# A six-layer transformer stack on one core: the score mask copied into PSUM by ScalarE, and a written order of half steps

## The chip, the cores and the metric

The kernel runs on one core of a Trainium2 chip. The core has five engines that run beside each other, each through its own queue in order: TensorE (PE in the profile, with PEld for its weight loads), VectorE (DVE), ScalarE (ACT), GpSimd (POOL) and SyncE (SP), which here only issues DMAs. Matmuls write to PSUM; DVE and ACT read and write PSUM and SBUF, POOL works in SBUF alone. The metric is the device time of the whole program in microseconds (us), smaller is better.

## The reference, cut to what matters

The input is `x` of 16 sequences, 256 tokens, 128 features, float32. First comes one causal attention layer with 16 heads of 8 features, added to `x` (called stage 1 below; the change does not touch it, apart from the constants that it prepares). Then a layernorm and a stack of six layers, whose result is added again:

```python
for i in range(6):
    x = attn_layer(shift_tokens(x), Wqkv[i], q_scale[i], k_scale[i], Wo[i]) + x
    x = ffn_layer(shift_tokens(x), ln_g[i], ln_b[i], W1[i], b1[i], W2[i], b2[i]) + x
```

`shift_tokens` takes half of the features from the token before. `attn_layer` has 16 heads of 64 features: queries and keys are divided by their norms, scaled and rotated (rotary tables with a decay), and each block of 32 tokens attends to itself and to the block before, under a mask:

```python
sim = einsum('bhwie,bhwje->bhwij', bq, bk2) * 8.0
sim = where(mask, -finfo.max, sim)
out = einsum('bhwij,bhwje->bhwie', softmax(sim, -1), bv2)
```

`ffn_layer` is a layernorm, a product with `W1` (128 to 682), a gated gelu and a product with `W2` (341 to 128). All matmuls of the stack are in float32.

## The kernel before, in words

**Work units.** The stack runs over `n = 16 * layer + sequence`, 96 values. For each `n` there are two half steps, `u = 0` and `u = 1`, each for half of the 16 heads. The function `half(n, u)` writes down one half step; 192 of them follow each other. It is a software pipeline: one half step holds parts of several `n` and of the feed-forward net (the "glu") of an earlier pair of sequences `m`. The glu works on two sequences at once and its parts are spread over four half steps, so the pattern repeats every four half steps. They are called here E0 (n even, u = 0), E1 (n even, u = 1), O0 and O1 (n odd).

**What a half step does.** Per half step, with `i, j` the two quarters of 4 heads that belong to `u`, and `b` the half of heads whose softmax weights are ready:

- `proj_qk` for `n + 2` (twice, each with q and k): two matmuls, ACT squares the result (L495), DVE multiplies by the rotary tables (L496, 128x1024). Then POOL adds the squares (L505) and the rotary halves (L508, two of 128x512), all behind the second of the pair.
- in u = 0: `norms` for `n + 1` (column sums of the squares, PE), an ACT copy, then `roots` (a PE transpose and a chain of 12 small DVE operations), POOL spreads the result (`kb`, L542).
- `spread_k` and `norm_k`, for two of four head groups each: PE transposes `kb` into PSUM, DVE scales the keys (L567, two), and SP issues four DMAs of 256 KB that lay q and k out anew (`us`, L569).
- `masks`: eight bf16 matmuls write the additive mask into the score tile in PSUM (L594), and `sim` adds the scores for four head groups onto it (L614, `start=False`). `soften` scales the scores and takes the row maximum (DVE, L626 and L634), and POOL subtracts it (L635).
- `power` takes the exponential (ACT, L641), half a step later `share` sums the rows and divides (DVE L648, L649; L651 on POOL, and on DVE where i is 1), `attn_T` transposes the weights (PE, L657) with an ACT copy (L659), `attn_v` multiplies by the values (PE, L677) with an ACT copy of the result (L686), and `project_out` closes the attention (PE L697, DVE L702).
- `proj_v` (PE L577, ACT L583), twice, with DMAs that lay the values out shifted by a block (`vs`, L584 and L586).
- glu: `glu_shift` (POOL), `glu_center`, `glu_var`, `glu_turn`, `glu_norm` and three `glu_part` (gelu on ACT, L797; product on DVE, L799), `glu_out` (PE L808, DVE L810).

**Order.** Each step function issues its instructions for all engines, and `in_order` then ties every PE, DVE, ACT and POOL instruction behind the one written before it on that engine. So each of the four engines runs exactly in the order in which `half` calls the steps. SP is not tied; the tile framework places the DMAs.

**Buffers.** PSUM has eight banks. Four are the pool `ps_o` (`psum1`): each result of a projection, transpose, norm or glu product takes one, and PE waits when all four are still to be read. The other four are two tiles of two banks (`ps_s`, `psum2`), which the scores and the attention result take in turn. In SBUF the buffers that matter are those with few copies: `t12` and `sq2` (2), `tq` (6), `us` and `sm` (3), `ao` and the value tiles (1 for each u), and the glu's scratch (1 each).

**Weights** of a layer are loaded at the step that first uses them: `load_qk` and `load_tables` (a DMA of 1 MB and two POOL operations, L436) in `proj_qk`, `load_v`, `load_out` and `load_glu` likewise.

Of the kernel before, what the change touches and what calls it, by code (L numbers as in the profile page):

```python
# [7 lines left out]
F32 = mybir.dt.float32  # L8
# [30 lines left out]
def tile_transformer(  # L39
# [35 lines left out]
    mask_b = const.tile([P, 2, 512], BF16, name="mask_b")  # L75
# [28 lines left out]
    with ExitStack() as st:  # L104
# [234 lines left out]
        def for_stack():  # L339

            for k in range(2):
                for half in range(2):
                    for quarter in range(4):
                        r = 32 * quarter
                        col = V_QK + 2 * k + (half + quarter) % 2
                        nc.gpsimd.tensor_copy(qks[r : r + 32, :, k, half], vecs[r : r + 32, :, col])

            nc.gpsimd.tensor_copy(
                mask_b.rearrange("p a n -> p (a n)"), cst1[:, C_MASK - C_CAUS : C_MASK - C_CAUS + 1024]
            )  # L350
# [36 lines left out]
    with ExitStack() as st:  # L387
# [13 lines left out]
        ps_s = st.enter_context(tc.tile_pool(name="ps_s", bufs=2, space=PSUM))  # L401
# [67 lines left out]
        xs, sq2s, t12s, sq, tq, us, rn, kbs, ao, sims, exs, aTs, pos, xns, hs = ({} for _ in range(15))  # L469
# [11 lines left out]
        def proj_qk(n, g, k):  # L481
# [20 lines left out]
            if k == 1:  # L502
                sq[n, g] = f5.tile([P, 2, S], F32, tag="sq", name=f"sq_{n}_{g}")
                tq[n, g] = e6.tile([P, 2, 2, S], F32, tag="tq", name=f"tq_{n}_{g}")
                nc.gpsimd.tensor_tensor(sq[n, g], sq2[:, :, 0, :], sq2[:, :, 1, :], ALU.add)  # L505

                for t in range(2):
                    nc.gpsimd.tensor_tensor(tq[n, g][:, t], t12[:, :, 0, t, :], t12[:, :, 1, 1 - t, :], ALU.add)  # L508
# [14 lines left out]
        def roots(n, n2):  # L523
# [16 lines left out]
            rn[n] = y  # L540
            kb = p1.tile([P, 2, NG, P], F32, tag="kb", name=f"kb_{n}")
# [46 lines left out]
        def masks(n, u):  # L588
            ps = sims[n, u] = psum2(f"sim_{n}_{u}")
            for r in range(4):  # L590
                for x in range(2):
                    w = 2 * x + r % 2
                    row = slice(32 * w, 32 * w + 32)
                    nc.tensor.matmul(  # L594
                        ps[WIN * r : WIN * r + WIN, x, :],
                        ident_b[row, row],
                        mask_b[row, 0 if r == 0 else 1, :],
                        start=True,
                        stop=False,
                        skip_group_check=True,  # L600
                    )

        def sim(n, u, g):


            ps, qk = sims[n, u], us[n, u]
            for h in range(2):
                for r in range(4):
                    c = block(r, h)
                    first = WIN if c == 0 else 0  # L610
                    col = 128 * g + 64 * h
                    for x in range(2):
                        part = slice(64 * x, 64 * x + 64)
                        nc.tensor.matmul(  # L614
                            ps[WIN * r : WIN * r + WIN, x, col + first : col + 64],
                            qk[part, g, 0, WIN * c : WIN * c + WIN],
                            qk[part, g, 1, WIN * (c - 1) + first : WIN * (c + 1)],
                            start=False,
                            stop=True,
                            skip_group_check=True,  # L620
                        )

        def soften(n, i):
            ps = sims[n, i // 2][:, i % 2]
# [9 lines left out]
            nc.vector.tensor_reduce(mx, seg, AX.X, ALU.max)  # L634
            nc.gpsimd.tensor_tensor(seg, seg, mx.unsqueeze(2).to_broadcast([P, 8, 64]), ALU.subtract)  # L635
            sms[n, i] = sm

        def power(n, i):
            sm = sms.pop((n, i))
# [4 lines left out]
        def share(n, i):  # L644
# [4 lines left out]
            nc.vector.reciprocal(rec, rec)  # L649
            on = nc.vector if i == 1 else nc.gpsimd  # L650
# [11 lines left out]
        def attn_v(n, i):  # L662
# [23 lines left out]
            nc.scalar.copy(ao[n, u][:, x], po[:, :, x])  # L686
# [17 lines left out]
        x2s, bcs, sms = {}, {}, {}  # L704
# [123 lines left out]
        def has(n):  # L828
            return 0 <= n < N
# [9 lines left out]

        def half(n, u):  # L840
            even = n % 2 == 0
            m = n // 2 - 1 if even else (n - 3) // 2
            glu = lambda m: 0 <= m < N // 2 - 1
# [3 lines left out]
            do(b, share, bi)  # L847
            do(b, share, bj)
            do(n, sim, u, 0)
            do(n, sim, u, 1)  # L850
            for k in range(2):
                do(n + 2, proj_qk, i, k)
            if u == 0:
                do(n + 1, sums)
            else:
                do(n + 1, spread_k, 1)
                do(n + 1, norm_k, 1)
                if not even and glu(m):
                    glu_norm(m)
            do(n, sim, u, 2)  # L860
            do(n, sim, u, 3)
            do(n, soften, i)
            do(n, soften, j)
            do(n - 1, project_out, u)
            if n == N - 1 and u:
                glu_shift((N // 2 - 1, 0))
            if u:
                do(n + 3, shift)
                if even and glu(m):
                    glu_shift(m)  # L870
            elif has(n + 1):
                roots(n + 1, n2s.pop(n + 1))
            do(b, attn_T, bi)
            do(b, attn_T, bj)
            do(n, proj_v, u, 0)
            do(b, attn_v, bi)
            if n == N - 1 and u:
                do(n, power, i)
                do(n, power, j)
            if not even and u == 0 and glu(m):  # L880
                glu_center(m)
            do(n + 2, proj_qk, j, 0)
            if even and u == 0 and glu(m - 1):
                glu_part(m - 1, 2)
            if not even and glu(m):
                if u == 0:
                    glu_var(m)
                else:
                    glu_part(m, 0)
                    glu_part(m, 1)  # L890
            do(n + 2, proj_qk, j, 1)
            if not even and u == 0 and glu(m):
                glu_turn(m)
            if u == 0:
                do(n + 1, spread_k, 0)
                do(n + 1, norm_k, 0)
            if n < N - 1 or u == 0:
                do(n, power, i)
                do(n, power, j)
            do(b, attn_v, bj)  # L900
            do(*((n, masks, 1) if u == 0 else (n + 1, masks, 0)))
            if even and u and glu(m - 1):
                glu_out(m - 1)
                if m - 1 >= (DEPTH - 1) * 8:
                    leave(2 * ((m - 1) % 8))
                    leave(2 * ((m - 1) % 8) + 1)
            do(n, proj_v, u, 1)

        def tail():
# [5 lines left out]
            share(n, 2)  # L915
            share(n, 3)
# [5 lines left out]
            attn_v(n, 2)  # L922
            attn_v(n, 3)
# [127 lines left out]
```

## Time and profile before

| what | value |
|---|---|
| three runs | 3608.91, 3615.72, 3619.88 us; median 3615.72 |
| span of the profiled execution, first to last instruction | 3608.7 us |
| stage 1 and the start of the stack, to the first mask of n = 0 | some 383 us |
| one period of four half steps in mid-stack (1600.03 to 1665.71) | 65.68 us |
| busy in that period: PE, DVE, POOL, ACT | 65.03, 54.19, 51.32, 36.19 us |
| granted TensorE clock | 0.990 over the span, 1.00 in that period |

No separate device time is listed for the profiled execution; its span is 0.2 us below the fastest of the three runs and 7.0 us below their median. [...] The chain of waits follows the work back from the last instruction, and in mid-stack its PE rows lie end to end, so that each row's length is what that group costs.

### The profile page before, as it was taken

To read this page: it belongs to the slowest core of one execution; us is meant where nothing else is said; L and a number is where in the kernel's file an instruction comes from. 1 tells how busy PE (TensorE), PEld (TensorE's weight loads), DVE (VectorE), ACT (ScalarE), POOL (GpSimd) and SP (SyncE) were. 2 spreads that over 40 slices of the span, in tenths; PEclk is the share of its full clock that TensorE was granted. 3 is DMA by queue.
4 is the path that set the end of the run, shared out by engine and by line. 5 is a ranking of instruction groups with operands and counts; after the bars stand their busy time and mean duration, and the time that the engine had idled before them with its cause. 6 is when DMAs were issued, how large, how long until landed. Compare 5 with 4: busy or idle time off the path is not lost.

```text
span 3608.7 us, 153932 instructions
## 1 busy us (share of the span) xinstructions
PE 3473.3 (96%) x68101; PEld 2428.7 (67%) x68101; DVE 2837.0 (79%) x4876; ACT 1881.1 (52%) x3184; POOL 2568.1 (71%) x2729
## 2 busy tenths in 40 slices
PE   8999799999999999999999999999999999999998
PEld 6777466666666666666666666666666666666665
DVE  6665788887888888888887888887888888888884
ACT  3444255554555555555555555555555555555553
POOL 2221787777777777787777777777777877777772
PEclk9999899999999999999999999999999999999999
DMA  3000333334433334333334333334433343443342
GB/s 83 10 9 10 97 94 98 99 95 104 112 104 86 92 100 112 102 105 101 84 96 119 105 90 100 95 90 120 111 92 87 100 110 86 109 107 93 101 105 63
DMA packets 249446, 331.69 MB, mean 92 GB/s; under 512 B 74446, under 2 KB 105548, under 8 KB 247884
## 3 DMA queue, kind: packets, MB, share of 16 engines
q1 hardware_dynamic: 248060, 321.14, 34.1%
q8 instruction: 537, 8.80, 1.0%
q14 instruction: 129, 1.06, 0.1%
q10 hardware_dynamic: 720, 0.70, 0.1%
HBM read 28.14 MB, written 4.19 MB: 9 GB/s over the span
## 4 chain that ended last, share of the span: by engine, by line
PE 78%; DVE 9%; issue 7%; POOL 3%; ACT 2%; DMA 1%; SPq 0%; POOLq 0%; DVEq 0%; ACTq 0%
PE qk L494 18%; PE po L677 11%; PE v L577 9%; PE wo L697 8%; PE sim L614 7%; PE w L808 4%; PE hg L794 3%; PE ha L795 3%; PE aT L657 3%; PE n L515 2%; DVE tq L567 2%; PE bc L553 2%; PE sim L594 2%; DVE t L496 2%; ACT aT L659 1%
## 5 line engine op out<-in xcount | busy, mean ns | idle before, releaser
L496 DVE TENSOR_TENSOR t<-qk,ab 128x1024 f32<-128x1024 f32 x768 | 916.6, 1219 | 277.1 <-ACT sq L495 244.9
L508 POOL TENSOR_TENSOR tq<-t 128x512 f32<-128x512 f32 x768 | 961.4, 1273 | 87.7 <-DVE t L496 69.5
L494 PE MATMUL qk<-xs,wqk 128*128 128x256 f32 x3072 | 792.6, 394 | 1.2 <-DVE yT L702 1.2
L505 POOL TENSOR_TENSOR sq<-sq 128x512 f32<-128x512 f32 x384 | 489.1, 1274 | 339.6 <-ACT sq L495 327.3
L494 PEld LDWEIGHTS qk<-xs,wqk 128*128 128x128 f32 x3072 | 555.5, 191 | 155.6 <-issue 54.9
L495 ACT ACTIVATE sq<-qk 128x512 f32<-128x512 f32 x768 | 459.5, 598 | 352.4 <-PE qk L494 346.8
L659 ACT COPY aT<-aT 128x512 f32<-128x512 f32 x384 | 207.7, 587 | 600.3 <-PE aT L657 599.9
L677 PEld LDWEIGHTS po<-aT,vs 64*64 64x64 f32 x12288 | 327.3, 134 | 201.5 <-issue 109.1
L577 PE MATMUL v<-wv,xs 128*128 128x512 f32 x768 | 422.9, 632 | 27.8 <-ACT aT L659 21.2
L635 POOL TENSOR_TENSOR sm<-sm,mx 128x512 f32<-128x512 f32 x384 | 396.3, 1043 | 30.4 <-DVE mx L634 29.8
L677 PE MATMUL po<-aT,vs 64*64 64x32 f32 x12288 | 393.8, 222 | 7.7 <-issue 4.3
L614 PEld LDWEIGHTS sim<-us 64*32 64x32 f32 x24576 | 262.5, 105 | 205.6 <-issue 190.5
L677 PE MATMUL po<-aT,vn 64*64 64x32 f32 x12288 | 386.0, 219 | 3.3 <-issue 3.3
L583 ACT COPY vn<-v 128x512 f32<-128x512 f32 x384 | 225.3, 587 | 312.1 <-PE v L577 307.6
L697 PE MATMUL wo<-ao,wout 128*128 128x256 f32 x1536 | 382.7, 392 | 0.0
L677 PEld LDWEIGHTS po<-aT,vn 64*64 64x64 f32 x12288 | 329.6, 135 | 5.2 <-issue 5.2
L614 PE MATMUL sim<-us 64*32 64x64 f32 (+1 forms) x24576 | 324.7, 221 | 3.6 <-DMA us<-tq 3.2
L651 POOL TENSOR_TENSOR ex<-ex,rec 128x512 f32<-128x512 f32 x288 | 296.4, 1043 | 42.6 <-DVE rec L649 22.0
L697 PEld LDWEIGHTS wo<-ao,wout 128*128 128x128 f32 x1536 | 276.0, 189 | 47.4 <-issue 0.2
L686 ACT COPY ao<-po 128x512 f32<-128x512 f32 x384 | 222.9, 580 | 118.2 <-PE po L677 117.9
L648 DVE TENSOR_REDUCE rec<-ex 128x8 f32<-128x512 f32 x384 | 252.1, 656 | 32.8 <-ACT ex L641 32.8
L634 DVE TENSOR_REDUCE mx<-sm 128x8 f32<-128x512 f32 x384 | 263.5, 686 | 13.3
(145 smaller groups left out, 5206.5 us busy)
## 6 DMA issues: line engine op xcount, KB each, us to landing
us<-tq SPq DMA_DIRECT2D x768, 256.0 KB
vs<-vn SPq DMA_DIRECT2D x384, 192.0 KB
vs<-vn SPq DMA_DIRECT2D x192, 64.0 KB
wqk<-in_f_wqkv_dram SPq DMA_DIRECT2D x96, 64.0 KB
ab<-in_tables_dram SPq DMA_DIRECT2D x6, 1024.0 KB
wv<-in_f_wqkv_dram SPq DMA_DIRECT2D x12, 256.0 KB
wout<-in_f_wo_dram SPq DMA_DIRECT2D x24, 128.0 KB
x<-in_x_dram SPq DMA_DIRECT2D x16, 128.0 KB
```

What stands on the lines that cost most here:

```text
L494: nc.tensor.matmul(ps[:, t * S : t * S + S], W["qk", g][:, k, t, :], xs[n], start=True, stop=True)
L495: nc.scalar.activation(sq2[:, k].rearrange("p t n -> p (t n)"), ps, AF.Square)
L496: nc.vector.tensor_tensor(t12[:, k].rearrange("p f t n -> p f (t n)"), ps.unsqueeze(1).to_broadcast([P, 2, 2 * S]), W["ab", l][:, k].rearr ...
L505: nc.gpsimd.tensor_tensor(sq[n, g], sq2[:, :, 0, :], sq2[:, :, 1, :], ALU.add)
L508: nc.gpsimd.tensor_tensor(tq[n, g][:, t], t12[:, :, 0, t, :], t12[:, :, 1, 1 - t, :], ALU.add)
L577: nc.tensor.matmul(ps, xs[n][:, P * c : P * c + P], W["v"][:, u].rearrange("p g x d -> p (g x d)"), start=True, stop=True)
L614: nc.tensor.matmul(ps[WIN * r : WIN * r + WIN, x, col + first : col + 64], qk[part, g, 0, WIN * c : WIN * c + WIN], qk[part, g, 1, WIN * ( ...
L634: nc.vector.tensor_reduce(mx, seg, AX.X, ALU.max)
L635: nc.gpsimd.tensor_tensor(seg, seg, mx.unsqueeze(2).to_broadcast([P, 8, 64]), ALU.subtract)
L651: on.tensor_tensor(seg, seg, rec.unsqueeze(2).to_broadcast([P, 8, 64]), ALU.mult)
L677: nc.tensor.matmul(po[DH * y : DH * y + DH, h, x, g, WIN * r : WIN * r + WIN], v[64 * h : 64 * h + 64, r // 2, 2 * g + y, x, :], aT[64 * h ...
L697: nc.tensor.matmul(ps[:, :S].rearrange("p (h m) -> p h m", h=2), W["out"][:, g, 2 * u + x, :], a[:, x, :, g, :], start=(j == 0), stop=(j == 3)
```

## The change

**The mask.** Before, eight bf16 matmuls of 32x32 by 512 wrote the mask for each half step. Now the score tile `simt` is one fixed PSUM tile of two banks. PE writes the mask into it once, at n = 0 and u = 0, by two identity matmuls; from then on ScalarE copies the mask (bf16 in SBUF, 128x512, read twice) into both banks, one instruction of 128x1024, and the score matmuls add to that as before. The attention result has the other two-bank tile by itself.

**The steps split.** `add_sq` and `add_t` (POOL) are now steps apart from `proj_qk`; `spread_rn` (POOL) apart from `roots`; `below` (POOL) apart from `soften`; `divide_by` apart from `share`; `evict` (the ACT copy) apart from `attn_v`. No instruction other than the mask is added or removed in the stack.

**The order.** Four strings, one for each of E0, E1, O0 and O1, give the order of the steps. The four score groups S0 to S3 stand in one run for PE, where before two stood before the first `proj_qk` and two after it.

```diff
-    mask_b = const.tile([P, 2, 512], BF16, name="mask_b")
+    mask_s = const.tile([P, 512], BF16, name="mask_s")
...
-        ps_s = st.enter_context(tc.tile_pool(name="ps_s", bufs=2, space=PSUM))
+        ps_s = st.enter_context(tc.tile_pool(name="ps_s", bufs=1, space=PSUM))
+        ps_m = st.enter_context(tc.tile_pool(name="ps_m", bufs=1, space=PSUM))
+
+        simt = ps_m.tile([P, 2, 512], F32, name="simt")
...
+        def add_sq(n, g):
+            sq2 = sq2s.pop((n, g))
+            sq[n, g] = f5.tile([P, 2, S], F32, tag="sq", name=f"sq_{n}_{g}")
+            nc.gpsimd.tensor_tensor(sq[n, g], sq2[:, :, 0, :], sq2[:, :, 1, :], ALU.add)
+
+        def add_t(n, g):
+            t12 = t12s.pop((n, g))
+            tq[n, g] = e6.tile([P, 2, 2, S], F32, tag="tq", name=f"tq_{n}_{g}")
+            for t in range(2):
+                nc.gpsimd.tensor_tensor(tq[n, g][:, t], t12[:, :, 0, t, :], t12[:, :, 1, 1 - t, :], ALU.add)
...
         def masks(n, u):
-            ps = sims[n, u] = psum2(f"sim_{n}_{u}")
-            for r in range(4):
+
+            if n == 0 and u == 0:
                 for x in range(2):
-                    w = 2 * x + r % 2
-                    row = slice(32 * w, 32 * w + 32)
-                    nc.tensor.matmul(
-                        ps[WIN * r : WIN * r + WIN, x, :],
-                        ident_b[row, row],
-                        mask_b[row, 0 if r == 0 else 1, :],
-                        start=True,
-                        stop=False,
-                        skip_group_check=True,
-                    )
+                    nc.tensor.matmul(simt[:, x], ident_b, mask_s, start=True, stop=True, skip_group_check=True)
+            else:
+                nc.scalar.copy(simt, mask_s.unsqueeze(1).to_broadcast([P, 2, 512]))
...
+        def below(n, i):
+            sm, mx = sms[n, i]
+            seg = sm.rearrange("p g h k -> p (g h) k")
             nc.gpsimd.tensor_tensor(seg, seg, mx.unsqueeze(2).to_broadcast([P, 8, 64]), ALU.subtract)
...
+        def divide_by(n, i):
+
+            seg = exs[n, i].rearrange("p g (h k) -> p (g h) k", h=2)
+            rec = recs.pop((n, i))
             on = nc.vector if i == 1 else nc.gpsimd
             on.tensor_tensor(seg, seg, rec.unsqueeze(2).to_broadcast([P, 8, 64]), ALU.mult)
...
+        def evict(n, i):
+            u, x = divmod(i, 2)
+            nc.scalar.copy(ao[n, u][:, x], pos[n, u][:, :, x])
...
+        ORDER = {
+            (0, 0): "WO SH1 SM1 Q0a SH0 SM0 Q0b NS S1 QT0 S2 S3 S0 SO1 AT1 RT AT0 V0 AV0 SB1 QA0 AC0 SO0 GP2 MK KB Q1a Q1b SB0 SK0 QA1 NK0 PW0 V1 QT1 AV1 PW1 AC1",
+            (0, 1): "SH1 SHF S1 S3 SH0 SM1 SM0 S2 S0 Q0a WO Q0b AT1 QT0 Q1a SO0 SO1 SK1 GS AT0 Q1b QA0 V0 AV0 QA1 AV1 V1 AC1 MK NK1 AC0 SB0 SB1 GO QT1 PW1 PW0",
+            (1, 0): "SH0 SM0 Q0a WO SH1 SM1 Q0b NS S0 S1 QT0 S2 S3 RT AT0 SO0 SO1 V0 GC AV0 GV AC0 KB SB0 AT1 QA0 Q1a SB1 Q1b AV1 AC1 QA1 V1 GT SK0 PW1 PW0 MK QT1 NK0",
+            (1, 1): "SH1 WO SH0 S3 S0 SM0 S1 S2 SM1 GN Q0a SO1 Q0b Q1a SO0 AT0 QT0 V0 SK1 AV0 AT1 SHF AC0 Q1b GP0 AV1 NK1 SB1 QA1 MK AC1 SB0 QA0 V1 QT1 GP1 PW1 PW0",
+        }
...
+            for step in ORDER[odd, u].split():
+                what[step]()
```

The names in the strings: SH `share`, SM `divide_by`, SO `soften`, SB `below`, PW `power`; S0 to S3 `sim`, MK `masks`; Q0a, Q0b (q and k of the first group) and Q1a, Q1b `proj_qk`, QA `add_sq`, QT `add_t`; NS `norms`, RT `roots`, KB `spread_rn`, SK `spread_k`, NK `norm_k` (with its four `us` DMAs); AT `attn_T`, AV `attn_v`, AC `evict`, WO `project_out`; V0, V1 `proj_v` (with the `vs` DMAs); SHF `shift`; GS, GC, GV, GT, GN, GP0 to GP2 and GO the glu's parts. The key (0, 0) is E0, (0, 1) E1, (1, 0) O0 and (1, 1) O1. The last half step runs in `tail`, which calls the split steps one after the other.

## The prediction

> **What bounds the kernel now.** First the page: busy shares, then the chain that ended last.
>
> ```profile
> PE 3473.3 (96%) x68101; PEld 2428.7 (67%) x68101; DVE 2837.0 (79%) x4876; ACT 1881.1 (52%) x3184; POOL 2568.1 (71%) x2729
> ...
> PE 78%; DVE 9%; issue 7%; POOL 3%; ACT 2%; DMA 1%; SPq 0%; POOLq 0%; DVEq 0%; ACTq 0%
> ```
>
> PE is the bound by both. Next one period of four half steps (table by windows), and the chain inside its E0.
>
> ```profile
> sum 65.68, PE 65.03 PEld 45.04 DVE 54.19 ACT 36.19 POOL 51.32; mean PE 16.26 PEld 11.26 DVE 13.55 ACT 9.05 POOL 12.83
> ```
>
> ```profile
> 1649.27 0.34 PE sim L594 x8
> 1649.61 1.05 PE v L577 x2
> 1650.66 0.77 PE sim L614 x40
> 1651.43 1.92 PE qk L494 x8
> 1653.35 1.00 PE n L515 x16
> 1654.35 0.77 PE sim L614 x41
> 1655.12 1.92 PE wo L697 x8
> ...
> 1657.74 0.60 ACT aT L659
> 1658.33 0.04 issue
> 1658.38 1.13 PE v L577 x2
> 1659.50 1.06 PE po L677 x64
> 1660.57 1.06 PE qk L494 x4
> ...
> 1663.34 0.86 PE qk L494 x4
> ```
>
> Three things are to be seen. The mask costs PE 0.34 us per half step. The same four qk matmuls cost 0.86 us behind a full-width group and 1.06 behind `po`; two pairs cost 1.92, not 1.72, behind `sim`. So each change from small tiles (sim, po, n, pv, mask) to full-width matmuls costs about 0.20. And PE stops once here: `v` has no free PSUM bank until ACT has copied `aT`.
>
> **PE's floor.** Adding the PE rows of the chain for E0, E1, O0, O1, with aT at 0.87 and v behind it at 0.86, gives 15.92 + 12.98 + 18.31 + 16.87 = 64.08; measured 65.68, so 1.60 of waits. The change takes away:
> - masks: 4 x 0.34 = 1.36 (8 instructions each).
> - changes from small to full: before 4 + 4 + 5 + 4 = 17 (mask to v or w, sim to qk, sim to wo, po to qk or cen, pv to qk). After: E0 S to AT1, AV0 to GP2; E1 S to Q0a, AV1 to V1; O0 S to RT, GV to AT1, AV1 to V1; O1 S to GN, AV0 to AT1, AV1 to V1; 10. 7 x 0.20 = 1.40. Four of the ten lead to transposes, which no row shows behind small tiles; I take 0.20 as for the others (0 to 0.20).
>
> New floor: 64.08 - 1.36 - 1.40 = 61.32. Before, DVE at 54.19 filled 83% of the period; now it fills 88%, POOL 84%, so the question is whether PE still gets its inputs.
>
> [...]
>
> **The mask on ACT.** No row has a 128x1024 copy. Bounds: one 128x512 copy, 0.59, and two of them back to back, 1.08 (aT, x2). The copies of 256 and 512 columns (0.37, 0.59) continue to 1.02; I take that. It waits for both `soften` reads, and Q1a's square, the exponentials, `vn` and `ao` copies queue behind it on ACT; the scores of the next half step wait for it.
>
> [...] If each mask had to stay on PE, the sum would be 46 x 1.36 = 63 us higher. [...]
>
> **The walk.** I lay the new strings out, each engine in its order, with the trace's distances: DVE t 1.13, soften 1.32, share 0.8, roots 3.87, norm_k 1.2, wo 0.37, h 0.7; POOL rotary 2.46, squares 1.24, sm, ex and kb 1.0 each; ACT 0.6, gelu 0.69, table load 1.28. Times run from each half step's PE start; the engines' backlogs are carried round until they repeat.
>
> *E0.* PE: WO 0, Q0 1.71, NS 3.43, scores 4.43 to 5.97, AT1, RT 6.60, AT0 6.82, V0 7.25, AV0 8.11, GP2 9.17, Q1 11.09, SK0 12.81, V1 13.25, AV1, end 15.17. DVE: yT 1.75, then solid: soften 6.05, roots 7.37 to 11.24, soften to 12.56, h to 13.26, two t, norm_k to 16.7. SM1 is ready at 4.1, SM0 at 6.0 (0.8 before AT0); kb at 12.35 (0.46 before SK0). ACT: mask 12.0 to 13.0, end 17.8. POOL ends at 18.0 with QT1.
>
> *E1.* PE: scores 0, Q0a 1.54, WO 2.60, Q0b, AT1 5.17, Q1a, SK1 6.46, AT0 6.90, Q1b, V0 8.19, AV0 9.05, AV1, V1 11.17, GO, end 14.79. WO needs `ao` of E0, free at 17.8 - 15.2 = 2.6: just there. DVE is solid from 2.0 to 12.9. The `vs` DMA of E0's V1 is queued on SP behind four `us` DMAs (3.02 to issue, about 5 to move by the DMA share after 1602) and lands near 8.0, 1 before AV0. POOL falls back to 18.4, ACT to 17.1.
>
> *O0.* PE: Q0a 0, WO, Q0b, NS 3.43, scores 4.43, RT 5.97, AT0 6.39, V0, GC, AV0, GV, AT1 9.95, Q1, AV1, V1 13.36, SK0 14.53, end 14.97. The key DMAs of E1's NK1 are all in by 18.6 - 14.8 = 3.8, before the scores. SM0 ready at 4.6. ACT: exponentials wait for POOL's SB1 (15.0), and the mask is behind them: done 17.2.
>
> *O1.* WO at 0, scores at 1.71, but the mask is done at 17.2 - 15.0 = 2.25: PE waits 0.5. Then GN, Q0, Q1a, AT0 7.0 (SM0 at 5.75), V0, SK1, AV0, AT1, Q1b, GP0 11.3, AV1, V1, GP1, end 16.85. DVE idles 1.7 for the gelu (table load 12.2 to 13.5) and catches up. POOL carries 2.5, ACT 2.7 into E0, as assumed there.
>
> So the PSUM stops of before (each two transposes in front of v) go; what is late next is the mask in O1 (0.55 with WO's bank) and margins under 1 us at SM0, kb, `ao` and `vs`. Each stop also bares a weight load, 0.2 (v 1.13 against 0.86 to 1.06); I add two. Period: 61.32 + 0.55 + 0.40 = 62.27, against 65.68: 3.41 less.
>
> Costed at nothing: the fixed score tile (before, scores and attention result took two tiles in turn, so each had one already; the copy is free to start when both `soften` are through); POOL's steps moved (SB, QA, QT, KB), which PE's row hides as long as the margins above last, else each costs its lateness; two constant copies for one in stage 1, where POOL is 20% busy.
>
> On SP the `us` DMAs now stand between the two `vs` groups in E0 and O1, and behind both in E1 and O0. That is counted for E0; in O1 the last `vs` lands 2.4 before AV0 of the next half step.
>
> **Layers.** Five times a layer begins. E0 took 20.11 there instead of 16.44, because POOL's table product, 3.74, ended 9.2 after its start and DVE's t waited. Now SH0 stands behind that t on DVE, so SM0 and AT0 are later by another 1.0. WO, which loads `wout` in O0, stands at 0.9 instead of some 7 us into the half step; the load was issued 0.7 us before that half step (950.82) and took 2.9 to issue: 0 to 5, I take 2.5. Together 5 x 3.5 = 17.5 worse. Start and tail: same work, 0 (a few us either way).
>
> **Sum.** 46 periods lie between 503 and 3530 us. 3608.7 - 46 x 3.41 + 17.5 = 3469 for the span. The profile's span stands 7.0 below the median of the runs: 3476.
>
> **The rivals.**
> 1. *The engines behind PE take half of it back* (chance 0.20). DVE runs solid from 1.75 in E0 to 12.9 in E1; 2% on its rows is 0.5 by then, more than kb's margin. Two or three further stops of 0.5 plus 0.2 in each period: 1.4 to 2.1, 65 to 97 us, so 3541 to 3573. For: before, PE stopped for DVE's norm_k (1608.29). Against: 7 us of slack for DVE in each period of the walk.
> 2. *Slower* (0.19): POOL in order becomes the bound of PE. QT1 (2.46) stands last, and its backlog of 2.5 to 4.8 lies in front of the next SM0 and SM1, for which AT waits, with AV and all of PE's row behind it. The margins are 0.8 to 2. The margins of the walk at SM0 are 0.8, 2.0, 1.8 and 1.3, mean 1.5. With POOL x later in every half step PE loses 4 (x - 1.5 + 0.2) per period; the gain of 3.41, less 0.38 for the layers, is used up at x = 2.06. At x = 2.6 the period is 2.2 longer than before: 3616 + 46 x 2.2 = 3717. For: POOL's rows are 1.0 to 2.5 long and cannot pass each other. Against: 51 of 62 us of load.
> 3. *The mask gains nothing* (in 1's chance): scores wait for ACT in each half step as in O1; 4 x 0.5 is 92 us, 3545 with the rest. Against: in E0, E1 and O0 the copy is done 1.7 to 8 us before the scores.
>
> **How the numbers follow.** Main case 0.58, its own range 3425 (no stop, floor 61.3, no layer loss) to 3525. Rival 1 and 3 0.20, to 3600. No change 0.03, slower 0.19. The range 3425 to 3605 holds main and rival cases, 0.78. About 0.3% is what a measurement of this kernel can tell: faster 0.78, same 0.03, slower 0.19.
>
> **What would show it.** The 0.34 rows gone; an ACT copy of 128x1024 of about 1.02; sim groups in one run of about 1.54, followed by one row 0.20 longer; a period near 62.3; waits of PE on `aT` copies (before 21.2 and 42.3 us at v) nearly gone; a wait of sim for ACT of some 0.5 in O1. Wrong it is if AT waits for POOL's ex, SK for kb, or po for the `vs` DMA in most half steps; or if the O0 at each layer's start is over 5 us longer.

## The result, and the profile after

| | median of 13 runs, us | lowest to highest | against before |
|---|---|---|---|
| before, same chip | 3611.64 | 3601.13 to 3619.88 | |
| after | 3622.39 | 3614.26 to 3628.38 | 1.0027 [1.0018, 1.0037] |

The change gained nothing: it is 11 us slower, inside the 0.3% that counts as no change by its middle, though not by the whole of its interval. The forecast was 3476. The profiled execution of after has a span of 3622.5 us.

The page of after, busy shares and the chain that ended last:

```profile
PE 3344.1 (92%) x66566; PEld 2400.0 (66%) x66567; DVE 2954.2 (82%) x4876; ACT 2059.1 (57%) x3377; POOL 2593.5 (72%) x2730
...
DVE 34%; PE 29%; POOL 21%; issue 11%; ACT 3%; DMA 1%; SPq 0%; POOLq 0%; DVEq 0%; ACTq 0%
```

PE has 129 us less work, as meant. But PE's share of the chain fell from 78% to 29%, and DVE and POOL took its place. DVE executes the same 4876 instructions as before and is busy for 117 us more. That is the first thing to ask about: no DVE instruction was added.

One period of four half steps in mid-stack, from E0's start (1598.44) to the next (table by windows):

```profile
sum 65.23, PE 61.93 PEld 44.14 DVE 56.87 ACT 39.83 POOL 51.91; mean PE 61.93 PEld 44.14 DVE 56.87 ACT 39.83 POOL 51.91
```

Before: 65.68 with PE 65.03 and DVE 54.19. So PE lost 3.1 us of work per period and gained 2.65 us of standing still. The rows of PE in that period in front of which it stood (timeline; the bracket is idle time and what ended it):

```profile
1613.02 0.66 PE L563 MATMUL bc<-cst,kb 128*128 128x128 f32 x4 [1.57 <-POOL kb L552]
1613.82 1.13 PE L587 MATMUL v<-wv,xs 128*128 128x512 f32 x2 [0.15 <-DVE h L814]
...
1646.16 0.63 PE L563 MATMUL bc<-cst,kb 128*128 128x128 f32 x4 [1.16 <-DVE t L499]
1647.20 1.99 PE L712 MATMUL wo<-ao,wout 128*128 128x256 f32 x8 [0.41 <-DVE t L499]
```

The first is SK0 in E0, which waits for POOL's `kb`; the third is SK0 in O0 and the fourth WO in O1, where no PSUM bank is free until DVE has done its `t`. Together 3.29 us of idling. Each stop also bares a weight load, which then no longer runs beside a matmul (0.14 us for `bc`, 0.19 for `v` and `wo` in PEld's rows): the four `bc` take 0.66 and 0.63 instead of 0.44, `v` 1.13 instead of 0.86, `wo` 1.99 instead of 1.73, so 0.94 more. The prediction's PE floor of 61.32 plus 3.29 plus 0.94 is 65.55; measured 65.23. The floor was right to 0.3. What was wrong is the waits.

Where does `kb` lose its time? The chain in E0, DVE's stretch (start, length):

```profile
1606.40 0.14 DVE nx L537
...
1606.56 1.17 DVE rn L541
...
1607.76 1.01 DVE nz L544
...
1608.79 1.20 DVE nz L545
...
1610.01 0.24 DVE rn L546
...
1610.27 0.24 DVE nz L544
```

and what POOL executes beside it (timeline):

```profile
1605.16 2.50 POOL L515 TENSOR_TENSOR tq<-t 128x512 f32<-128x512 f32 x2
1607.61 1.05 POOL L643 TENSOR_TENSOR sm<-sm,mx 128x512 f32<-128x512 f32 x1
1608.61 1.27 POOL L509 TENSOR_TENSOR sq<-sq 128x512 f32<-128x512 f32 x1
1611.92 1.04 POOL L552 COPY kb<-rn 128x1024 f32<-128x1024 f32 x1 [2.04 <-DVE rn L546]
```

These DVE operations are all of 64 elements a partition. Three of them take 1.0 to 1.2 us, the rest 0.23, and the same line (L544) appears with both lengths. The long ones end where a POOL operation ends: 1607.73 beside 1607.66, 1608.77 beside 1608.66, 1609.99 beside 1609.88. After 1609.88 POOL has nothing left that it may do, because KB waits for this very chain, and from then on each operation takes 0.23. This is no chance of one period: on these four lines (L541, L544 to L546) 231 of the 960 operations of the whole trace took longer than 0.3 us, and every one of the 231 ended 0.05 to 0.09 us after the end of a POOL instruction. The chain (eleven operations; the twelve of the description above is one too many) took 5.5 us here (1606.32 to 1611.8) and 4.8 in O0; the prediction's walk had 3.87 for both.

The trace of before shows the same thing, smaller. DVE's timeline in that chain:

```profile
1658.72 0.74 DVE L534 TENSOR_SCALAR rn<-nx 128x64 int32<-128x64 int32 x1
1659.49 0.99 DVE L537 TENSOR_TENSOR nz<-nx,rn 128x64 f32<-128x64 f32 x1
1660.52 0.22 DVE L538 SCALAR_TENSOR_TENSOR nz<-nz,rn 128x64 f32<-128x64 f32 x1
```

and POOL's beside it:

```profile
1658.37 2.04 POOL L635 TENSOR_TENSOR sm<-sm,mx 128x512 f32<-128x512 f32 x2
1662.69 1.04 POOL L542 COPY kb<-rn 128x1024 f32<-128x1024 f32 x1 [2.29 <-DVE rn L539]
```

Two operations were held there, until the two POOL operations were through (1660.41). The new order puts three POOL steps (QT0, SB1, QA0) in front of KB in E0, so there is more for the chain to be held by. The groups by line of before (count, then busy time and mean ns of one):

```profile
L537 DVE TENSOR_TENSOR nz<-nx,rn 128x64 f32<-128x64 f32 x288 | 136.7, 475 | 10.1 <-DMA wv<-in_f_wqkv_dram 0.2
...
L538 DVE SCALAR_TENSOR_TENSOR nz<-nz,rn 128x64 f32<-128x64 f32 x288 | 66.3, 230 | 9.9
...
L534 DVE TENSOR_SCALAR rn<-nx 128x64 int32<-128x64 int32 x96 | 59.1, 616 | 3.3
```

and the same three in after:

```profile
L544 DVE TENSOR_TENSOR nz<-nx,rn 128x64 f32<-128x64 f32 x288 | 148.4, 515 | 10.1 <-DVE rn L541 0.2
...
L545 DVE SCALAR_TENSOR_TENSOR nz<-nz,rn 128x64 f32<-128x64 f32 x288 | 108.9, 378 | 9.9
...
L541 DVE TENSOR_SCALAR rn<-nx 128x64 int32<-128x64 int32 x96 | 104.6, 1090 | 3.3
```

These three lines alone are 100 of DVE's 117 additional us (11.7 + 42.6 + 45.5). The division on DVE (its mean went from 1001 to 1226 ns), which also has both inputs in SBUF, adds 22; the sum is over 117 because neighbouring operations overlap by up to 0.1 us in the timeline. L544 and L545 have two inputs in SBUF: 0.23 us alone, and 0.96 to 1.24 where they were held (94 and 46 of 288 each). L541 has only one input in SBUF and is held all the same: 90 of 96 times, 0.57 to 1.24 us. What in the hardware holds them is not shown by any run here.

### The profile page after: what moved, and what is told of

Read it like the earlier page. It is cut to its first block, busy times and chain, and to the rows that moved or that the text cites. A ratio compares the mean times of both kernels' runs of the same rounds, so it can differ in the third digit from the quotient of the medians.

```text
span 3622.5 us, 150845 instructions
## 1 busy us (share of the span) xinstructions
PE 3344.1 (92%) x66566; PEld 2400.0 (66%) x66567; DVE 2954.2 (82%) x4876; ACT 2059.1 (57%) x3377; POOL 2593.5 (72%) x2730
## 4 chain that ended last, share of the span: by engine, by line
DVE 34%; PE 29%; POOL 21%; issue 11%; ACT 3%; DMA 1%; SPq 0%; POOLq 0%; DVEq 0%; ACTq 0%
DVE t L499 11%; POOL tq L515 8%; PE wo L712 6%; PE qk L497 6%; POOL sq L509 5%; PE simt L617 5%; DVE nz L544 4%; POOL sm L643 4%; DVE sm L629 4%; DVE nz L545 3%; PE po L690 3%; DVE rn L541 3%; PE v L587 3%; DVE rec L655 2%; DVE mx L637 2%
## 5 line engine op out<-in xcount | busy, mean ns | idle before, releaser
L497 PE MATMUL qk<-xs,wqk 128*128 128x256 f32 x3072 | 762.3, 383 | 6.2 <-issue 3.9
L509 POOL TENSOR_TENSOR sq<-sq 128x512 f32<-128x512 f32 x384 | 486.5, 1272 | 28.5 <-ACT sq L498 24.8
L664 POOL TENSOR_TENSOR ex<-ex,rec 128x512 f32<-128x512 f32 x288 | 322.7, 1121 | 133.2 <-DVE rec L656 126.2
L712 PE MATMUL wo<-ao,wout 128*128 128x256 f32 x1536 | 371.6, 385 | 22.5 <-DVE t L499 18.8
L672 ACT COPY aT<-aT 128x512 f32<-128x512 f32 x384 | 225.5, 587 | 291.1 <-PE aT L670 290.2
L712 PEld LDWEIGHTS wo<-ao,wout 128*128 128x128 f32 x1536 | 290.1, 192 | 93.6 <-DVE t L499 30.0
L617 PE MATMUL simt<-us 64*32 64x64 f32 (+1 forms) x24576 | 298.9, 224 | 44.3 <-issue 33.5
L617 PEld LDWEIGHTS simt<-us 64*32 64x32 f32 x24576 | 259.0, 106 | 111.9 <-issue 76.2
L648 ACT ACTIVATE ex<-sm 128x512 f32<-128x512 f32 x384 | 226.6, 625 | 119.2 <-POOL sm L643 118.2
```

Of the source, the lines that this page charges most:

```text
L497: nc.tensor.matmul(ps[:, t * S : t * S + S], W["qk", g][:, k, t, :], xs[n], start=True, stop=True)
L617: nc.tensor.matmul(ps[WIN * r : WIN * r + WIN, x, col + first : col + 64], qk[part, g, 0, WIN * c : WIN * c + WIN], qk[part, g, 1, WIN * ( ...
L712: nc.tensor.matmul(ps[:, :S].rearrange("p (h m) -> p h m", h=2), W["out"][:, g, 2 * u + x, :], a[:, x, :, g, :], start=(j == 0), stop=(j == 3)
```

## The experiments

Theory A: the chain of `roots` is held up by POOL's work beside it, it became longer in the new order, and PE waits for what comes behind it; without that the new order gives what the forecast said. Rivals: the mask on ACT is what stops PE (the prediction's third); POOL's load or order is the bound whatever DVE does (its second); the new order's length has to do with something else.

**1. The roots' scratch in PSUM, in the order after and in the order before.** `x` and `z` move into unused columns of the PSUM bank that holds the transposed norms, so that every operation of the chain has at most one input in SBUF, and L541, which had one, has none. Nothing else changes; the number of instructions is the same.

```diff
-            ps = psum1(f"nT_{n}").rearrange("p (h g m) -> p h g m", h=4, g=4)
+            nT = psum1(f"nT_{n}")
+            ps = nT.rearrange("p (h g m) -> p h g m", h=4, g=4)
...
-            x = p2.tile([P, 2, NG, 8], F32, tag="nx", name=f"nx_{n}")
+            x_, z = nT[:, 256:320], nT[:, 320:384]
+            x = x_.rearrange("p (h g m) -> p h g m", h=2, g=NG)
...
-            x_, y_ = (v.rearrange("p h g m -> p (h g m)") for v in (x, y))
+            y_ = y.rearrange("p h g m -> p (h g m)")
             for _ in range(3):
-                z = p4.tile([P, 64], F32, tag="nz", name=f"nz_{n}")
```

In the order after:

> The changed kernel; in the root chain x and z lie in PSUM (spare columns of the bank of nT), so that each DVE operation of the chain has at most one input in SBUF. Nothing is left out. Theory A (the chain of small DVE operations is held up by POOL operations that run beside it, and passes this on to PE through kb and the PSUM banks): the chain, now about 5.4 us in E0 and 4.8 in O0, shrinks to 3.1 to 3.5; the waits of PE for kb (1.6 per period) and for the rotary product in front of bc and wo (1.6 per period) fall to under 0.5 each; 3480 to 3540 us. Rival B (DVE and POOL are simply full in this order, and the banks late): the chain may shorten, but the same waits come back elsewhere; 3595 to 3625.

Measured: 3461.82 us against 3613.32 of before on the same chip, 0.9588 [0.9567, 0.9609]. The page's chain:

```profile
PE 76%; issue 7%; POOL 6%; ACT 4%; DVE 4%; DMA 2%; SPq 0%; POOLq 0%; DVEq 0%; ACTq 0%
```

the groups of the root operations:

```profile
L545 DVE TENSOR_TENSOR nT<-nT,rn 128x64 f32<-128x64 f32 x288 | 66.9, 232 | 9.9
L546 DVE SCALAR_TENSOR_TENSOR nT<-nT,rn 128x64 f32<-128x64 f32 x288 | 66.8, 232 | 10.0
...
L543 DVE TENSOR_SCALAR rn<-nT 128x64 int32<-128x64 int32 x96 | 21.6, 225 | 3.4
```

and PE's wait for `kb` over the whole span (total us, times, longest; in after it is 70.2, 48, 3.9):

```profile
PE bc L564 <- POOL kb L553: 9.7, 4, 5.9
```

All root operations take 0.23 with POOL working beside them (its `tq` and `sm` last 2.50 and 1.04 as before, so only DVE had paid). The chain takes 2.9 us, PE is the bound again, and 161 us are gained on after. That is more than was expected of this run; 2.9 is also less than the 3.87 of the walk.

In the order before:

> The kernel before with the same edit of the root chain. Theory A: before, PE is the bound and the chain (about 4 us, two of its operations held up) has cover; at most 0.5 us per period from the shorter hold of banks: 3585 to 3612. Rival B: the same. If it gains over 50 us, the edit helps by itself and says nothing of the change.

Measured: 3607.73, 0.9984 [0.9974, 0.9994]. DVE loses 103 us of busy time (2837.0 to 2733.7; in the new order 218, 2954.2 to 2736.3), and almost nothing follows: there the chain of roots stood beside PE's work and not in front of it (PE waited 14.6 us for `kb` in before, 70.2 in after). The same edit is worth 161 us behind the new order and about 6 in front of it.

**2. Each half of the change by itself.** First the old order with the mask copied by ACT (the score tile fixed, as in after):

```diff
         def masks(n, u):
-            ps = sims[n, u] = psum2(f"sim_{n}_{u}")
-            for r in range(4):
...
+            if n == 0 and u == 0:
+                for x in range(2):
+                    nc.tensor.matmul(simt[:, x], ident_b, mask_s, start=True, stop=True, skip_group_check=True)
+            else:
+                nc.scalar.copy(simt, mask_s.unsqueeze(1).to_broadcast([P, 2, 512]))
```

> The order of before, with the mask copied by ScalarE into one fixed score tile, at the place where PE wrote it. Per period PE saves 1.36 us (63 us in all, 3550) if the copy is always in time. But in this order the scores stand 1.05 us behind the mask step; the copy is behind two exponentials and an ao copy on ACT and would end some 1.6 us late at E0 to E1 and O1 to E0: theory A expects the gain to go there, 3580 to 3650. The rival, that moving the mask is worth its PE time in any order: 3540 to 3560.

Measured: 3845.99, 1.0647 [1.0631, 1.0663], far above what was expected. PE's wait for the mask:

```profile
PE simt L610 <- ACT simt L597: 229.6, 143, 2.5
```

and that of its weight loads:

```profile
PEld simt L610 <- ACT simt L597: 349.5, 144, 3.3
```

The first score group stands at the start of the half step in that order, and the mask behind two exponentials and the copy of the attention result on ACT: it ended at 1647.49 in one half step, where ACT's queue had been solid since 1644.35. In three half steps of four PE stands still for it, up to 2.5 us. So the prediction's third rival is true of the old order. Part of the 233 us is not the waiting itself: at the end of many of these stops the granted clock stands at half for 3.4 or 6.8 us, and the same eight matmuls take twice as long. Two rows of the chain, the second with a granted clock of 0.50 from 1665.8 to 1672.6:

```profile
1648.38 1.92 PE qk L497 x8
...
1667.73 3.71 PE qk L497 x8
```

Between 520 and 3500 us the clock stands at half for 225 us in this run and for 14 in before. Half of the difference, 105 us, is an upper estimate of what that costs.

Then the new order with the mask written by PE's eight matmuls, at the place of MK:

```diff
         def masks(n, u):
-            if n == 0 and u == 0:
-                for x in range(2):
-                    nc.tensor.matmul(simt[:, x], ident_b, mask_s, start=True, stop=True, skip_group_check=True)
-            else:
-                nc.scalar.copy(simt, mask_s.unsqueeze(1).to_broadcast([P, 2, 512]))
+            ps = simt
+            for r in range(4):
...
+                    nc.tensor.matmul(
+                        ps[WIN * r : WIN * r + WIN, x, :],
+                        ident_b[row, row],
+                        mask_b[row, 0 if r == 0 else 1, :],
```

> The changed kernel with its new order, but the mask written by eight PE matmuls per half step as before, at the step MK. Theory A: PE has 3 us of waits per period in the new order, which take up part of the 1.36 us that come back: 3625 to 3680. Rival C (the copy on ACT, and what queues behind it, is what costs the gain): 3540 to 3600.

Measured: 3722.39, 1.0308 [1.0291, 1.0324]; expected too low. PE waits:

```profile
PE simt L604 <- DVE sm L636: 123.7, 46, 5.4
```

Once a period, in E0, MK on PE waits for `soften` to have read the tile, and `soften` stands behind the held-up roots on DVE. Here too the clock is at half for 119 us of that stretch, which is up to some 53 us of the loss. So neither half gains alone: they are 233 and 109 us worse, and both together 11.

**3. Three more tests of the hold-up.** The first leaves the scratch in SBUF and changes only POOL's order: in E0 and O0 the steps that stood in front of KB beside the roots go behind it.

```diff
-            (0, 0): "... NS S1 QT0 S2 S3 S0 SO1 AT1 RT AT0 V0 AV0 SB1 QA0 AC0 SO0 GP2 MK KB Q1a ..."
+            (0, 0): "... NS S1 S2 S3 S0 SO1 AT1 RT AT0 V0 AV0 AC0 SO0 GP2 MK KB QT0 SB1 QA0 Q1a ..."
...
-            (1, 0): "... NS S0 S1 QT0 S2 S3 RT ... AC0 KB SB0 ..."
+            (1, 0): "... NS S0 S1 S2 S3 RT ... AC0 KB QT0 SB0 ..."
```

> The kernel after with its roots in SBUF as they are; only POOL's order differs: in E0 and O0 QT0 (and in E0 SB1 and QA0 as well) stands behind KB, so that POOL waits for the roots instead of working beside them. Theory A (the small DVE operations with two inputs in SBUF each last until the POOL operation beside them ends): the rows that now take 0.99 to 1.19 in E0 take about 0.23, the chain of roots falls from 5.5 and 4.8 to about 3, and `bc` no longer waits 1.57 for kb. POOL pays for it with up to 3 us of idling in E0 and in O0, on 51 of 62 us of load, and later `t12` buffers: 3450 to 3590. Theory B (the rows are long by themselves in this order, and PSUM placement cured it by other means): the rows keep 0.99 to 1.19 and the time is 3620 or more.

Measured: 3598.1, 0.9969 [0.9957, 0.998], above theory A's range and under theory B's. DVE's group of the operation that was held first (mean 1090 ns in after):

```profile
L541 DVE TENSOR_SCALAR rn<-nx 128x64 int32<-128x64 int32 x96 | 18.7, 195 | 3.3
```

and the wait of PE's weight loads for the mask (17.9, 48, 1.4 in after):

```profile
PEld simt L617 <- ACT simt L604: 104.0, 48, 3.3
```

Theory A's part on the operations holds: with POOL idle, the same code with the same SBUF operands runs at 0.2 us each and `bc` is on time. But POOL now stands still while the chain runs (4.02 us in E0, 2.79 in O0) and the time hardly moves: the exponentials come late behind POOL's SB1, the mask behind them, and O1's scores wait for it. PE's WO waits 39.5 us for ACT's `ao` copies as well (3.5 in after).

The second takes the length out of the chain and leaves the hold-up in: one Newton step in place of three. Two thirds of that refinement are left out.

```diff
-            for _ in range(3):
+            for _ in range(1):
```

> The kernel after with one Newton step in `roots` instead of three: two thirds of that computation are left out, so norms are coarse. Roots stay in SBUF and POOL beside them. The operations left out are six of 0.23 to 0.5, so the chain is 1.4 to 2 us shorter while its first operations stay held up. Theory A: it is the length of the chain that PE waits for, whatever shortens it. The wait of 1.57 for kb in E0 and most of the 1.16 and 0.41 behind DVE's t in O0 and O1 go; the period falls from 65.2 to 62.3 to 63, time 3460 to 3520. Theory C (moving x and z to PSUM helped POOL or something else, not the chain): 3560 or more. The first operations of the chain stay at 0.9 to 1.2 by either.

Measured: 3483.71, 0.9655 [0.9636, 0.9674]. The first operations are still held:

```profile
L544 DVE TENSOR_TENSOR nz<-nx,rn 128x64 f32<-128x64 f32 x96 | 105.3, 1097 | 3.5 <-DVE rn L541 0.2
...
L541 DVE TENSOR_SCALAR rn<-nx 128x64 int32<-128x64 int32 x96 | 104.9, 1093 | 3.3
```

and yet PE's waits for `kb` shrink from 70.2 us to 3.0. So it is the length of the chain that PE waits for, by whatever means it is shortened. PSUM did not help in some other way. This run is also the nearest test of the prediction's walk: with its first operations still held, the chain takes 3.92 us in E0 and 3.26 in O0 (medians of the trace), close to the 3.87 that the walk has, and the shortest periods take 62.05 to 62.13, where the forecast had 62.27.

The third asks whether the order alone could have spared the loss. Scratch in SBUF, POOL beside the roots, and two steps moved that the kernel with roots in PSUM pointed to (below):

```diff
-            (1, 0): "... V1 GT SK0 PW1 PW0 MK QT1 NK0",
+            (1, 0): "... V1 GT SK0 MK PW1 PW0 QT1 NK0",
-            (1, 1): "... AC0 Q1b GP0 AV1 NK1 SB1 ...",
+            (1, 1): "... AC0 Q1b NK1 GP0 AV1 SB1 ...",
```

> The kernel after, roots in SBUF and POOL beside them, with the two moves of the kernel with the second order (in O0 MK before PW1 and PW0, in O1 NK1 before GP0). It asks whether the order alone could have spared the loss. Theory A: the chain of roots stays at 5.5 and 4.8, PE still waits for kb in E0 and for DVE's t in O0, and the period of 65.2 hardly falls: 3590 to 3630. If the waits for kb and t were only a sequel of the late mask and the late keys: 3450 to 3530.

Measured: 3616.87, 1.0015 [1.0001, 1.0029]. The waits for `kb` and for `t` are as in after:

```profile
PE bc L563 <- POOL kb L552: 72.8, 48, 3.0
PE bc L563 <- DVE t L499: 42.5, 41, 1.5
```

The same two moves on the kernel in which POOL stands still:

> The kernel in which POOL stands still beside the roots (SBUF), with the same two moves. Without them its period was 65.2 again, although its root rows were back at 0.23, and PE waited 2 us and more for the mask in O1, which stood behind two exponentials that waited for POOL's SB1. Theory A: that wait was the whole of what held it, a second cost of POOL's order and not of the roots; with the mask in front of the exponentials the period falls to 62 to 63.5 and the time to 3440 to 3530. If POOL's own load with its idling (51 of 65 us and some 5 of idling) is the limit, the time stays at 3570 to 3600.

Measured: 3555.37, 0.9841 [0.9823, 0.9858], between the two cases: the late mask had been part of what held that kernel, not the whole. POOL's wait for the roots (in after 192.7, 87, 5.2):

```profile
POOL kb L552 <- DVE rn L546: 313.8, 90, 5.9
```

that of PE's weight loads for POOL's division (24.8 us in after), and the two longest of PE's matmuls:

```profile
PEld aT L670 <- POOL ex L664: 75.3, 93, 5.5
...
PE aT L670 <- POOL ex L664: 45.5, 54, 5.1
PE wo L712 <- ACT ao L701: 41.3, 32, 1.7
```

With the same two moves and the scratch in PSUM (test 5 below) the last two are 17.7 and 4.1 us. POOL idles 3.5 us in front of each KB and is behind later. It is late with the softmax weights, so `attn_T` waits. It is also late with the subtraction, for which the exponentials on ACT wait (2.31 us in one E0), and the `ao` copy behind them is late for WO. That is the prediction's second rival, POOL in order as the bound, and it comes into force when POOL is made to stand still for DVE. Taking the hold-up away by POOL's order costs most of what it brings; taking it away by where the operands lie costs nothing (0.23 us an operation in test 1).

**4. What the mask's move is worth once the roots are out of the way.** The kernel with roots in PSUM, and the mask on PE again (both edits above):

> The kernel after with x and z of the roots in PSUM, and the mask written by eight PE matmuls at the place of MK, as before the change. Against the same kernel with ACT's mask (3461.82) it prices the mask by itself, once the chain of roots is out of the way. By the prediction's sum 46 x 1.36 = 63 us for the rows, less about 25 for the wait of O1's scores on ACT, plus 0 to 0.5 per half step where MK on PE waits for `soften`: 3490 to 3590. Theory A': the mask's move is worth 1 to 2% only in this order. Rival: the mask on PE is hidden in waits that PE has anyway (under 3475).

Measured: 3524.31, 0.976 [0.9745, 0.9775], which is 62.5 us above the same kernel with ACT's mask. The prediction's sum has 46 x 1.36 = 62.6 for it. That the two agree to 0.1 is chance: by their intervals the two medians are known to 5 and 8 us, and they were taken on different chips. Two more things are inside the difference and nearly cancel. The mask on PE brings back three changes from small tiles to full-width matmuls (behind it `w` takes 2.77 instead of 2.58, `wo` 1.93 and `qk` 1.92 instead of 1.73), some 27 us in 46 periods; and only ACT's mask has the wait of O1's scores, some 25 (0.33 of idling and a bared weight load of 0.2). In quarter-point periods (table below) the mask's move is worth 1.24 us.

**5. A version that beats both.** In the kernel with roots in PSUM two stops were seen in the period that was read. O1's scores waited for the mask (45 times in the whole trace); it stood on ACT behind the copy `vn` and two exponentials, and in that period these waited for PE's `v` and not for POOL. And E0's scores waited 0.59 for a key DMA of O1's NK1, which stood behind GP0's product; this one shows in 13 periods only. The PE row of the first:

```profile
1637.77 1.54 PE L618 MATMUL simt<-us 64*32 64x32 f32 x128 [0.33 <-ACT simt L605]
```

With the two moves of the diff above:

> The kernel after with x and z in PSUM, and two steps moved: in O0 MK stands before PW1 and PW0, so that the mask does not wait behind vn and two exponentials which wait for POOL; in O1 NK1 stands before GP0, so that its key DMAs start some 1.5 us earlier. Left over in the kernel with roots in PSUM were a wait of O1's first scores for ACT (0.33 and a bare weight load, after an idle of about 0.5) and 0.59 of E0's scores for a us DMA. If these are all that PE still waits for: 46 x 0.5 to 1.3 less than 3461.8, so 3400 to 3440. If what moves later takes their place (the exponentials in O1, gelu's h behind norm_k): 3450 to 3475.

Measured: 3443.35, 0.9544 [0.9523, 0.9564], 3 us above the range that was named for the case that nothing takes the place of the two waits. The page's chain is PE's again:

```profile
PE 84%; issue 7%; POOL 4%; DVE 3%; DMA 1%; ACT 1%; SPq 0%; POOLq 0%; DVEq 0%; ACTq 0%
```

and in a stretch of mid-stack, 1600 to 1661, PE is busy for 60.70 of 61 us (table by windows):

```profile
sum 61.00, PE 60.70 PEld 43.80 DVE 50.72 ACT 38.83 POOL 51.50; mean PE 60.70 PEld 43.80 DVE 50.72 ACT 38.83 POOL 51.50
```

Last, the rotary tables of the next layer are loaded and scaled in the middle of a layer:

```diff
...
-                if g == 0:
+                if g == 0 and l == 0:
                     load_tables(l)
+                    scale_tables(l, 0)
+                    scale_tables(l, 1)
+            if k == 0 and g == 0 and l < DEPTH - 1:
+                if s == 6:
+                    load_tables(l + 1)
+                if s in (9, 11):
+                    scale_tables(l + 1, (s - 9) // 2)
```

> The kernel with x and z in PSUM and the second order, and the rotary tables of the next layer loaded and scaled in the middle of the layer (the DMA at its sequence 6, the two products on POOL at sequences 9 and 11) instead of at its start. At the starts of layers the period was 64.5 to 67.4 instead of 61 to 62, with the chain of waits through POOL's two table products and what stood behind them. Five times 2 to 4 us less than 3443: 3420 to 3435. If the starts are held by the weights' DMAs or by something else: 3438 to 3450.

Measured: 3434.8, 0.9512 [0.9497, 0.9527]. That is the fastest kernel here, 4.9% below before. What the tables alone bring (8.5 us) is hardly more than the intervals, which reach 5 to 7 us to either side, and the mean period fell only from 62.78 to 62.69, so that a gain by the tables is not shown.

The periods side by side, from one `glu_norm` product on DVE to the next (the first 45 distances of each profiled execution; a quarter of them are shorter than the quarter point):

| kernel | quarter point | mean | time, us |
|---|---|---|---|
| before | 65.58 | 66.57 | 3611.64 |
| after | 65.24 | 66.80 | 3622.39 |
| after, POOL idle beside the roots | 65.18 | 66.15 | 3598.1 |
| after, one Newton step | 62.75 | 63.86 | 3483.71 |
| after, roots in PSUM, mask on PE | 63.10 | 64.39 | 3524.31 |
| after, roots in PSUM | 61.86 | 63.21 | 3461.82 |
| the same, two steps moved | 61.52 | 62.78 | 3443.35 |

## Why the prediction was wrong

**The step that failed** is the term "roots 3.87" of the walk. It was read off the trace of before, where the two chains of a period take 3.85 and 4.09 (medians), and carried into the new order as if it were the price of its operations. By themselves they cost 2.9 (roots in PSUM); the rest is time in which POOL held them, and that depends on what POOL has to do just then: 1.0 and 1.2 in before, 2.6 in E0 and 1.9 in O0 of after. With it failed a term that was put at nothing: the moved POOL steps were to cost only their own lateness, and QT0, SB1 and QA0, which now stand beside the roots, made DVE's chain longer. In the walk `kb` was done 0.46 before SK0. It came 2.17 later than the walk had it, relative to E0's start (14.52 instead of 12.35): 1.6 from the chain itself and 0.5 because the chain began later. Less the margin that is 1.7, and PE stood 1.57. In O0 the chain was 0.9 longer, which made DVE's `t` late, and with it the PSUM banks for SK0 and WO (1.16 and 0.41). The prediction allowed 0.55 of stops and 0.40 of bared loads; there were 3.29 and 0.94. Less the 0.3 by which the floor was too high, the difference is 3.0 per period, 138 us in 46 periods, of the 146 by which the median was missed. The kernel with one Newton step, whose chain is about as long as the walk had it, takes 3483.71, 8 us from the forecast.

The trace of before had shown it: L537 and L538 are operations of one size in one loop, and their means were 475 and 230 ns.

**PE's floor of 61.32** was right to 0.3: the shortest periods of the kernel with two steps moved, where almost nothing waits, take 61.0. Both items in it hold. The 0.34 rows are gone (their price by difference, 62.5 us against 62.6, holds other things as well, see test 4). The changes from small tiles to full-width matmuls show in the kernel with roots in PSUM: `qk` behind `simt` 1.07 and behind a full group 0.86; `v` behind `po` 1.07 and 0.86; the two transposes `nT` behind `simt` 0.37 and behind `aT` 0.22; `aT` behind `po` 0.59 and 0.44. So 0.21 for matmuls and 0.15 for transposes, where 0.20 was taken for all, with 0 to 0.20 as bounds for the latter; 0.15 for the four transposes puts the floor at 61.1.

**The mask on ACT**: 1.02 predicted, 1.018 measured, with the bounds 0.59 to 1.08. No mask had to stay on PE after the first: ACT copied the 191 that followed. The group in after:

```profile
L604 ACT CAST simt<-mask_s 128x1024 f32<-128x1024 bf16 x191 | 194.5, 1018 | 86.1 <-DVE sm L629 86.1
```

The stop predicted for O1's scores (0.5) did not show in after, because PE came later than the mask there; with the roots out of the way it was there, in O1 and nowhere else, and cost about that.

**The walk** was right where the roots do not reach: E1 14.56 (14.79 in the walk), O1 16.47 (16.85). E0 and O0, which hold the roots, took 17.5 and 16.7 instead of 15.17 and 14.97. With the chain shortened the mean period fell by 3.36 against before (63.21 and 66.57); the prediction had 3.41 less 0.38 for the layers. Its 3476 is 14 us from the 3461.82 that the kernel with roots in PSUM takes; but there the chain is 1 us shorter than the walk's, and one of the stops (the key DMA) is not the walk's, so part of that nearness is luck.

**Layers.** 17.5 us worse was the estimate. By the table's periods, what lies above the quiet ones came to some 44 us in 45 periods before (66.57 against 65.6) and 72 after (66.80 against 65.2): 28 worse. Too low by 10, and the cause inside those periods was not tried apart beyond the tables.

**The rivals.** The first named the place, `kb`'s margin in E0 and DVE's rows, and thought of 2%; DVE's busy time in the period grew by 4.9% (54.19 to 56.87). It put the end at 3541 to 3573, with two or three stops of 0.5; there were four, with 1.57 the largest. Among the signs that would prove the forecast wrong the prediction listed SK waiting for `kb` in most half steps: that is the one that came, 48 times, which is once a period and was enough. The second rival (POOL in order) did not decide after, but did where POOL was made to wait. The third is true of the old order only.

## What to carry to other kernels

Before a chain of small DVE operations is priced from a trace, compare the means of operations of one size: where they differ, look whether the long ones end where a POOL instruction ends (here 231 of 231, by 0.05 to 0.09 us). If they do, the price holds for the old order only: here the chain went from 4.09 us to 5.5 in E0 and from 3.85 to 4.8 in O0 when other POOL steps stood beside it. Move the scratch inputs of such operations from SBUF to PSUM when a bank has columns to spare; here it cost nothing (0.23 us an operation either way), and it is worth something only when the chain is on the path, so the same edit gave 0.2% in one order and 4.4% in the other. When the bound of an engine is lowered by 5%, look again at every margin below a microsecond on the engines behind it, since those decide how much of the gain arrives.

## What the runs showed of the hardware that was not expected

A 0.23 us operation of 64 elements a partition on DVE took up to 1.24 us beside POOL in after. Each held one (231 of 960) ended 0.05 to 0.09 us after a POOL instruction, and two or three in a row were held in that way, until POOL ran out of work. With the scratch in PSUM none of the chain's operations took more than 0.23, with POOL's rows unchanged; with an idle POOL none did either. An operation with a single input in SBUF (L541) was held like those with two, 90 of its 96 times.

The granted TensorE clock fell to half in stretches of 3.4 or 6.8 us behind stops of PE. Between 520 and 3400 us there are 46 such stretches with ACT's mask in the old order (mean clock of the whole span 0.963), 33 with PE's mask in the new one (0.977), 15 in after with the two moves (0.984), 8 in after (0.989) and 3 in the kernel with roots in PSUM (0.992). Each of these begins within 2 us of the end of a stop of over 1.4 us. Not every such stop has one: there are 82, 55, 47, 47 and 16 of them. In before there are 4 stretches, two of them behind no such stop. What decides was not tried.
